# A Mamba block's last chunk finished row tile by row tile, and the graph attention's first adjacency loaded ahead of its branch

## The chip, the cores and the metric

The kernel runs on one core of a Trainium2 chip. The metric is the device time of one execution in microseconds (us); lower is better. The core has TensorE (PE, with its weight loads shown apart as PEld), VectorE (DVE), ScalarE (ACT), GpSimd (POOL) and SyncE (SP), whose queue issues the transfers from memory. Each engine works through its own instructions in order and waits for others by semaphores.

## What is computed

Four graph layers over n = 3327 nodes with 256 features, each of the form x = layernorm(x + layer(x, adj)). All is float32. The second layer (a graph convolution followed by a Mamba scan) and the third (graph attention) are the two between which the change lies:

```python
# layer 1
h = layernorm(relu(adj @ x @ gcn_w + gcn_b))
xz = h @ w_in;  xc, z = xz[:, :512], xz[:, 512:]
u = silu(causal_conv4(xc));  dt, B, C from u @ w_xp
h_t = exp(dt*A) * h_(t-1) + dt*B*u          # a scan over the 3327 nodes, 16 states
y = (h_t @ C + u * D_skip) * silu(z)
x = layernorm(x + y @ w_out)
# layer 2
h = x @ W.T;  a_src = (h*attn_src).sum(-1);  a_dst = (h*attn_dst).sum(-1)
s = leaky_relu(a_src[None, :] + a_dst[:, None], 0.2) * (adj > 0)
w = softmax of s over the neighbours only
x = layernorm(x + elu(w @ h))
```

Layer 0 is an aggregation with a linear map. Layer 3 runs two steps of diffusion with the adjacency and of a bilinear attention (queries and keys of 64 features) that keeps the top 0.9 of each row's probability.

## The kernel before

The nodes are padded to 3328, that is 26 row tiles of 128. X holds the features of all tiles in SBUF for the whole run, F is a second array of the same size that holds the layer's values, and col holds each node's two attention terms. A tile framework places the buffers, sets the semaphores, and orders each engine's instructions; memory of a closed pool is used again by later pools, and an instruction that writes into such memory waits for its last users.

**The Mamba block.** The scan runs over chunks of up to 512 nodes (WC), four row tiles in the last one. For each of 16 states, `decay`, `feed` and `scan` work on ScalarE, GpSimd and VectorE, and TensorE sums the states in PSUM (line 557). The function `gate` (489 to 491) multiplies the sum with the gate. `back` (493 to 519) then finishes a chunk: for each row tile a matmul with w_out in four parts (line 502), the residual into X (504) and its statistics (505, lines 84 and 85 of the helper); then one reciprocal root for the tiles of the chunk on GpSimd (`power`, lines 249 and 250, and 509, 510), and the normalization on ScalarE (514). For all chunks but the last this lies beside the scan of the next chunk. For the last, lines 575 to 579 run it to its end, and then `values` (332 to 350) for its four tiles: two transposes of X (341), a copy (343), the product with the attention's weights (346), and from it col (347) and F (349, 350). Sums, transposes and products all use the two PSUM buffers "ps" of one pool.

**The graph attention** has two forms. Lines 675 to 709 prepare it: they test whether the scores are small enough for the fast form (`fit`), compute q, eps and r, and a branch at 754 chooses `layer2` (711 to 752) or `layer2_any`. In `layer2` each of the 26 rows of tiles comes in two halves of 13 tiles (JH): a load of the transposed adjacency (724), the weights w as a maximum of r and q (726), the mask (729), which writes the weighted half into the load's buffer, and 13 matmuls (732). Each float32 matmul stands as two records in the trace. The row is finished by 737 to 751, the last step on GpSimd (L593, L594, L751), and `project` of the row before (L101, L103, and L600, L602, L604 in `key_and_query`) makes its key and query; the query goes to memory (qd, line 606).

**The last layer** begins behind the branch with loads of U1 and U2 (763) and of the rows ln3 (764), of queries (1108) and of adjacency thirds (807, in `aggregated`), the scores (793), a search for each row on VectorE, and the diffusion's matmuls (809). Some of these loads do not depend on the attention, and where their memory is free they are issued before the branch.

Of the kernel before, what the change touches and what calls it, by code (L numbers as in the profile page):

```python
# [9 lines left out]
F32 = mybir.dt.float32  # L10
BF16 = mybir.dt.bfloat16
I32 = mybir.dt.int32
AF = mybir.ActivationFunctionType
ALU = mybir.AluOpType
# [4 lines left out]
P = 128  # L19
D = 256  # L20
EPS = 1e-5
JH = 13
J0 = 4
JC = 9
WC = 512
DI = 512
NG = DI // P
# [16 lines left out]
def gnn_kernel(ctx: ExitStack, tc: tile.TileContext, n: int, a: dict, out: bass.AP):  # L44
    nc = tc.nc
    nt = -(-n // P)
# [35 lines left out]
    def stats(mv, y):  # L82
        st = small.tile([P, 6], F32, name="bnst")
        nc.vector.bn_stats(st, y)  # L84
        nc.vector.bn_aggr(mv, st)
# [68 lines left out]
    with tc.tile_pool(name="l1b", bufs=1) as wpool, tc.tile_pool(name="l1at", bufs=2) as l1at:  # L154
        X0 = F[:, :, :D]
# [32 lines left out]
        with tc.tile_pool(name="l1aw", bufs=1) as cwork, tc.tile_pool(name="l1c", bufs=2) as ch, \  # L188
# [58 lines left out]
            def power(rs, var):  # L247

                nc.gpsimd.tensor_scalar(rs, var, EPS, None, op0=ALU.add)
                nc.gpsimd.tensor_tensor(rs, rs, mhalf[:, :var.shape[1]], op=ALU.pow)  # L250
# [237 lines left out]
            def gate(c, ys):  # L488
                sz = szs[c]
                for g in range(NG):  # L490
                    nc.vector.tensor_mul(sz[:, g, :], ys[g][:, :sz.shape[2]], sz[:, g, :])

            def back(c):

                sz = szs[c]
                m = sz.shape[2] // P
                mv = small.tile([P, WC // P, 2], F32, name="mvc")
                for i in range(m):
                    it = starts[c] // P + i
                    po = psum.tile([P, WC], F32, name="ps")[:, :D]  # L500
                    for g in range(NG):
                        nc.tensor.matmul(po, sz[:, g, i * P:(i + 1) * P], w_out[:, g, :],
                                         start=(g == 0), stop=(g == NG - 1))
                    nc.vector.tensor_add(X[:, it, :], X0[:, it, :], po)
                    stats(mv[:, i, :], X[:, it, :])
                rs = small.tile([P, WC // P], F32, name="rsc")
                power(rs[:, :m], mv[:, :m, 1])
                nb = small.tile([P, WC // P], F32, name="nbc")
                nc.gpsimd.tensor_tensor(nb[:, :m], mv[:, :m, 0], rs[:, :m], op=ALU.mult)
                nc.gpsimd.tensor_scalar(nb[:, :m], nb[:, :m], -1.0, None, op0=ALU.mult)  # L510
                yield
                for i in range(m):
                    it = starts[c] // P + i
                    x = nc.scalar.activation(X[:, it, :], X[:, it, :], AF.Identity, scale=rs[:, i:i + 1], bias=nb[:, i:i + 1])
                    if i == 0:
                        tc.keep_in_program_order(x)
                nonlocal ready
                ready = ends[c] // P
                yield
# [53 lines left out]
                if c + 1 < nch:  # L573
                    x = y
            gate(nch - 1, ys)
            for _ in back(nch - 1):
                pass
            while valued < nt:
                values()

# [3 lines left out]
    with tc.tile_pool(name="l3", bufs=1) as pool, tc.tile_pool(name="l3d", bufs=1, space=DRAM) as dram:  # L584
# [89 lines left out]

        with tc.tile_pool(name="l2c", bufs=1) as cpool:
            fit = cpool.tile([1, 1], I32, name="fit")
            with tc.tile_pool(name="l2a", bufs=1) as wpool, \
                    tc.tile_pool(name="l2p", bufs=3, space=PSUM) as psum:

                big = wpool.tile([P, nt, 2], F32, name="big")  # L680
                nc.scalar.activation(big, col, AF.Abs)
                m = wpool.tile([P, 2], F32, name="m")
                nc.vector.reduce_max(m, big.rearrange("p t k -> p k t"), axis=AX.X)
                pm = psum.tile([2, P], F32, name="ps")
                nc.tensor.transpose(pm, m, ident)
                m2 = wpool.tile([2, 1], F32, name="m2")
                nc.vector.reduce_max(m2, pm, axis=AX.X)
                one = wpool.tile([2, 1], F32, name="one")
                nc.vector.memset(one, 1.0)
                ps = psum.tile([1, 1], F32, name="ps")  # L690
                nc.tensor.matmul(ps, m2, one, start=True, stop=True)
                f = wpool.tile([1, 1], F32, name="f")
                nc.vector.tensor_scalar(f, ps, BIG, None, op0=ALU.is_le)
                nc.vector.tensor_copy(fit, f)

                q = cpool.tile([P, nt], F32, name="q")
                nc.scalar.activation(q, col[:, :, 0], AF.Exp, scale=0.8)
                eps = cpool.tile([P, nt], F32, name="eps")
                nc.scalar.activation(eps, col[:, :, 1], AF.Exp, scale=-1.0)
                nc.vector.tensor_scalar_mul(eps, eps, 1e-8)  # L700

                r = cpool.tile([P, npad], F32, name="r")
                for j0 in range(0, nt, 4):
                    m = min(4, nt - j0)
                    pt = psum.tile([P, 4, P], F32, name="ps")
                    for j in range(m):
                        nc.tensor.transpose(pt[:, j, :], col[:, j0 + j, 1:2].to_broadcast([P, P]), ident)
                    nc.scalar.activation(r[:, j0 * P:(j0 + m) * P], pt[:, :m, :].rearrange("p a b -> p (a b)"),
                                         AF.Exp, scale=-0.8)

            def layer2():
                with tc.tile_pool(name="l2", bufs=1) as pool, tc.tile_pool(name="l2w", bufs=2) as work, \
                        tc.tile_pool(name="l2at", bufs=5) as atp, \
                        tc.tile_pool(name="l2p", bufs=3, space=PSUM) as psum:
                    def project(it):
                        xt = transposed(work, psum, X[:, it, :], "xt")
                        key_and_query(work, psum.tile([P, P], F32, name="ps"), 0, it, xt)

                    for it in range(nt):
                        acc = psum.tile([P, D + 1], F32, name="acc")  # L720
                        for j0 in range(0, nt, JH):
                            m = min(JH, nt - j0)
                            at = atp.tile([P, JH, P], F32, name="at")
                            nc.sync.dma_start(at[:, :m, :], a["adjT"][it][:, j0:j0 + m, :])
                            w = work.tile([P, JH, P], F32, name="w", bufs=1)
                            nc.vector.tensor_tensor(
                                w[:, :m, :], r[:, None, it * P:(it + 1) * P].to_broadcast([P, m, P]),
                                q[:, j0:j0 + m, None].to_broadcast([P, m, P]), op=ALU.max)
                            nc.vector.scalar_tensor_tensor(at[:, :m, :], at[:, :m, :], 0.0, w[:, :m, :],  # L729
                                                           op0=ALU.is_gt, op1=ALU.mult)  # L730
                            for j in range(m):
                                nc.tensor.matmul(acc, at[:, j, :], F[:, j0 + j, :],  # L732
                                                 start=(j0 + j == 0), stop=(j0 + j == nt - 1))
                        if it:
                            project(it - 1)
                        den = small.tile([P, 1], F32, name="den")
                        nc.vector.tensor_add(den, acc[:, D:], eps[:, it:it + 1])
                        nc.vector.reciprocal(den, den)

                        ex = work.tile([P, D], F32, name="ex")  # L740
                        nc.vector.tensor_scalar(ex, acc[:, :D], den, 0.0, op0=ALU.mult, op1=ALU.min)
                        nc.scalar.activation(ex, ex, AF.Exp)
                        o = work.tile([P, D], F32, name="o")
                        nc.scalar.activation(o, acc[:, :D], AF.Relu, scale=den)
                        nc.vector.scalar_tensor_tensor(o, ex, -1.0, o, op0=ALU.add, op1=ALU.add)
                        nc.vector.tensor_add(o, o, X[:, it, :])
                        mv = small.tile([P, 2], F32, name="mv")
                        stats(mv, o)
                        rs = small.tile([P, 1], F32, name="rs")
                        power(rs, mv)  # L750
                        nc.gpsimd.tensor_scalar(X[:, it, :], o, mv[:, 0:1], rs, op0=ALU.subtract, op1=ALU.mult)  # L751
                    project(nt - 1)

            with tc.If(nc.values_load(fit[0:1, 0:1]) > 0) as small_scores:
                layer2()
            with small_scores.Else():
                layer2_any()
# [573 lines left out]
```

## Time and profile before

| | |
|---|---|
| device time, median of 3 | 3858.1 us (3853.97 to 3861.62) |
| span of the profiled execution | 3854.7 us |
| first matmul of the last chunk's w_out | 1617.68 us |
| last col of `values` | 1641.42 us |
| first attention matmul (L732) | 1652.72 us |
| last L600 of the attention starts | 1988.46 us |
| first diffusion matmul of the last layer (L809) | 1992.59 us |

A line of the timeline has the start and the duration in us, the engine, the source line, the operation, "output <- inputs" with shapes, and in brackets how long the engine had been idle before it and what ended that. A line of the waits has who waited for whom, the total in us, how often, and the longest. A line of the windows has the stretch, its length, the busy time of PE, PEld, DVE, ACT and POOL with the number of instructions, the clock that was granted to TensorE (1.00 is full), the share of the DMA engines and GB/s.

### The profile page before, as it was taken

To read this page: it belongs to the slowest core of one execution; us is meant where nothing else is said; L and a number is where in the kernel's file an instruction comes from. 1 tells how busy PE (TensorE), PEld (TensorE's weight loads), DVE (VectorE), ACT (ScalarE), POOL (GpSimd) and SP (SyncE) were. 2 spreads that over 40 slices of the span, in tenths; PEclk is the share of its full clock that TensorE was granted. 3 is DMA by queue.
4 is the path that set the end of the run, shared out by engine and by line. 5 is a ranking of instruction groups with operands and counts; after the bars stand their busy time and mean duration, and the time that the engine had idled before them with its cause. 6 is when DMAs were issued, how large, how long until landed. Compare 5 with 4: busy or idle time off the path is not lost. (4 is left out here: it accounts for less than half of the span.)

```text
span 3854.7 us, 41751 instructions
## 1 busy us (share of the span) xinstructions
PE 3499.9 (91%) x15079; PEld 2593.0 (67%) x15079; DVE 2610.2 (68%) x5588; ACT 1738.5 (45%) x2612; POOL 494.7 (13%) x734
## 2 busy tenths in 40 slices
PE   8999999898889778689989999999999999999975
PEld 7888876554554434378868787777777667667664
DVE  1111579898988999877753445444454888888987
ACT  0000665554545465211122333333346777777773
POOL 0000122222221221111110000000001111111110
PEclk9999999998999888889999999999999999999997
DMA  7443211111111000044423222122203112221100
GB/s 231 139 134 95 84 59 53 37 46 36 42 36 36 6 0 0 15 158 139 148 73 88 62 61 56 51 59 62 59 11 101 58 56 63 64 63 54 58 23 7
DMA packets 100529, 252.96 MB, mean 66 GB/s; under 512 B 14786, under 2 KB 49090, under 8 KB 100178
## 3 DMA queue, kind: packets, MB, share of 16 engines
q1 hardware_dynamic: 100306, 250.13, 21.2%
q8 instruction: 122, 2.00, 0.2%
q14 instruction: 101, 0.83, 0.1%
HBM read 239.86 MB, written 10.22 MB: 65 GB/s over the span
## 5 line engine op out<-in xcount | busy, mean ns | idle before, releaser
L473 DVE TENSOR_TENSOR_SCAN h<-dA,db 128x2052 f32<-128x2052 f32 (+3 forms) x128 | 464.0, 3625 | 5.9 <-PE y L557 3.4
L460 ACT ACTIVATE dA<-dt,A_log 128x512 f32<-128x512 f32 (+3 forms) x512 | 297.0, 637 | 326.7 <-DVE h L473 272.7
L557 PE MATMUL y<-h,ident 128*128 128x512 f32 (+3 forms) x1024 | 436.1, 563 | 3.2 <-DVE h L549 3.2
L841 PE MATMUL acc<-G,wt 128*128 128x256 f32 x1352 | 332.7, 396 | 63.4 <-ACT wt L839 62.2
L557 PEld LDWEIGHTS y<-h,ident 128*128 128x128 f32 x1024 | 199.4, 207 | 258.0 <-issue 232.4
L839 ACT COPY wt<-tp 128x512 f32<-128x512 f32 (+1 forms) x364 | 185.9, 554 | 382.7 <-PE tp L837 382.4
L841 PE MATMUL acc<-X,wt 128*128 128x256 f32 x1352 | 343.8, 391 | 10.3 <-ACT wt L839 9.8
L841 PEld LDWEIGHTS acc<-G,wt 128*128 128x128 f32 x1352 | 254.1, 194 | 133.7 <-ACT wt L839 81.6
L809 PE MATMUL acc<-F,at 128*128 128x256 f32 x1352 | 323.1, 389 | 0.6 <-ACT q L604 0.6
L116 PE MATMUL acc<-xa,at 128*128 128x257 f32 x1352 | 310.1, 383 | 5.4 <-DMA at<-in_adjT 5.4
L841 PEld LDWEIGHTS acc<-X,wt 128*128 128x128 f32 x1352 | 242.3, 189 | 105.5 <-issue 41.3
L732 PE MATMUL acc<-F,at 128*128 128x257 f32 x1352 | 307.9, 384 | 4.9 <-DVE at L729 4.9
L264 PE MATMUL cb<-F,at 128*128 128x256 f32 x1352 | 310.6, 382 | 1.6 <-ACT hn L283 1.6
L809 PE MATMUL acc<-X,at 128*128 128x256 f32 x1352 | 309.4, 383 | 2.9 <-issue 2.9
L809 PEld LDWEIGHTS acc<-F,at 128*128 128x128 f32 x1352 | 253.8, 193 | 74.0 <-issue 40.0
L264 PEld LDWEIGHTS cb<-F,at 128*128 128x128 f32 x1352 | 257.3, 191 | 58.7 <-issue 17.7
L466 DVE TENSOR_TENSOR db<-du,row 128x2048 f32<-128x2048 f32 (+3 forms) x128 | 240.2, 1879 | 82.6 <-ACT row L448 82.5
L853 DVE MAX8 cand<-e 128x8 f32<-128x128 f32 x676 | 142.2, 281 | 226.4 <-ACT e L795 214.9
L116 PEld LDWEIGHTS acc<-xa,at 128*128 128x128 f32 x1352 | 256.7, 192 | 42.6 <-issue 5.4
L809 PEld LDWEIGHTS acc<-X,at 128*128 128x128 f32 x1352 | 255.0, 192 | 44.0 <-issue 10.9
L732 PEld LDWEIGHTS acc<-F,at 128*128 128x128 f32 x1352 | 256.4, 193 | 41.8 <-issue 5.1
L549 DVE TENSOR_TENSOR h<-h,C 128x2048 f32<-128x2048 f32 (+3 forms) x128 | 240.9, 1882 | 37.2 <-PE C L484 23.7
(305 smaller groups left out, 5303.6 us busy)
## 6 DMA issues: line engine op xcount, KB each, us to landing
at<-in_adjT SPq DMA_DIRECT2D x102, 832.0 KB, 4.5
at<-in_adjT SPq DMA_DIRECT2D x156, 448.0 KB, 3.4
at<-in_adjT SPq DMA_DIRECT2D x52, 576.0 KB, 3.8
at<-in_adjT SPq DMA_DIRECT2D x52, 320.0 KB, 3.0
at<-in_adjT SPq DMA_DIRECT2D x26, 512.0 KB, 3.5
xt<-in_xT SPq DMA_DIRECT2D x26, 128.0 KB, 4.1
qd<-q SPq DMA_DIRECT2D x104, 32.0 KB, 1.9
q<-qd SPq DMA_DIRECT2D x52, 64.0 KB, 2.3
```

The lines of the kernel that those rows point to most:

```text
L116: nc.tensor.matmul(acc, at[:, j, :], rhs[:, j0 + j, :], start=(j0 + j == 0), stop=(j0 + j == nt - 1))
L264: nc.tensor.matmul(acc, at[:, j % JC, :], X0[:, j, :], start=(j == 0), stop=(j == nt - 1))
L460: nc.scalar.activation(dA[:, g, 1:], dt[:, g, :], AF.Exp, scale=A[:, g, s:s + 1])
L466: nc.vector.tensor_mul(by_group(dbs[s % 2], w)[:, :, 1:], du, B.to_broadcast([P, NG, w]))
L473: nc.vector.tensor_tensor_scan(h[:, :m], dAs[s % 2][:, :m], dbs[s % 2][:, :m], initial=0.0, op0=ALU.mult, op1=ALU.add)
L549: nc.vector.tensor_mul(h, h, C.to_broadcast([P, NG, w]))
L557: nc.tensor.matmul(ys[g][:, :w], ident, h[:, g, :], start=False, stop=(s == DS - 1))
L732: nc.tensor.matmul(acc, at[:, j, :], F[:, j0 + j, :], start=(j0 + j == 0), stop=(j0 + j == nt - 1))
L809: nc.tensor.matmul(acc, at[:, j, :], rhs[:, j0 + j, :], start=(j0 + j == 0), stop=(j0 + j == nt - 1))
L839: nc.scalar.copy(wt[:, :m, :], pt[:, :m, :])
L841: nc.tensor.matmul(acc, wt[:, j, :], rhs[:, j0 + j, :], start=(j0 + j == 0), stop=(j0 + j == nt - 1))
L853: nc.vector.max(cand[:, s * 8:(s + 1) * 8], z[:, s * SEG:(s + 1) * SEG])
```

## The change

It has two parts. The last chunk is no longer finished by `back`: a loop takes each row tile through its sum, statistics, reciprocal root and normalization by itself, with `values` of the tile before it in between, so that a tile need not wait for the other three. And the two halves of the attention's first row of adjacency get buffers of their own, at0 and at13, in the pool that is open before the branch, and are loaded there; row 0 uses them, and the pool for the other rows has four buffers instead of five. The sum of a tile has become a function of its own, which `back` uses too.

```diff
+            def residual(c, i):
+                it = starts[c] // P + i
+                po = psum.tile([P, WC], F32, name="ps")[:, :D]
+                for g in range(NG):
+                    nc.tensor.matmul(po, szs[c][:, g, i * P:(i + 1) * P], w_out[:, g, :],
+                                     start=(g == 0), stop=(g == NG - 1))
+                nc.vector.tensor_add(X[:, it, :], X0[:, it, :], po)
...
             gate(nch - 1, ys)
-            for _ in back(nch - 1):
-                pass
+            for i in range(us[nch - 1].shape[2] // P):
+                it = starts[nch - 1] // P + i
+                residual(nch - 1, i)
+                mv = small.tile([P, 2], F32, name="mv")
+                stats(mv, X[:, it, :])
+                rs, nb = (small.tile([P, 1], F32, name=x) for x in ("rs", "nb"))
+                power(rs, mv[:, 1:2])
+                nc.gpsimd.tensor_scalar(nb, mv[:, 0:1], rs, -1.0, op0=ALU.mult, op1=ALU.mult)
+                nc.scalar.activation(X[:, it, :], X[:, it, :], AF.Identity, scale=rs, bias=nb)
+                while valued < ready:
+                    values()
+                ready = it + 1
             while valued < nt:
                 values()
...
             fit = cpool.tile([1, 1], I32, name="fit")
+            ats = [cpool.tile([P, min(JH, nt - j0), P], F32, name=f"at{j0}") for j0 in range(0, nt, JH)]
+            for k, at in enumerate(ats):
+                nc.sync.dma_start(at, a["adjT"][0][:, k * JH:k * JH + at.shape[1], :])
...
-                        tc.tile_pool(name="l2at", bufs=5) as atp, \
+                        tc.tile_pool(name="l2at", bufs=4) as atp, \
...
-                            at = atp.tile([P, JH, P], F32, name="at")
-                            nc.sync.dma_start(at[:, :m, :], a["adjT"][it][:, j0:j0 + m, :])
+                            if it:
+                                at = atp.tile([P, JH, P], F32, name="at")
+                                nc.sync.dma_start(at[:, :m, :], a["adjT"][it][:, j0:j0 + m, :])
+                            else:
+                                at = ats[j0 // JH]
```

More of the change, by code (lines that the diff above doesn't have):

```diff
@@ L491, in gate @@
                     nc.vector.tensor_mul(sz[:, g, :], ys[g][:, :sz.shape[2]], sz[:, g, :])
+            def residual(c, i):
[5 more added lines that the diff above has]
+                nc.vector.tensor_add(X[:, it, :], X0[:, it, :], po)
             def back(c):
-                sz = szs[c]
-                m = sz.shape[2] // P
+                m = szs[c].shape[2] // P
                 mv = small.tile([P, WC // P, 2], F32, name="mvc")
                 for i in range(m):
[L499 to L505, printed above, removed]
+                    residual(c, i)
+                    stats(mv[:, i, :], X[:, starts[c] // P + i, :])
                 rs = small.tile([P, WC // P], F32, name="rsc")
```

## The prediction

> **What bounds the kernel now.** I read the busy table first, then the chain of waits, then the waits of TensorE alone from the change to the end of the graph attention (1624 to 1990 us), then the timeline around each of them, and last the windows of 1 us with the granted clock.
>
> ```profile
> PE 3499.9 (91%) x15079; PEld 2593.0 (67%) x15079; DVE 2610.2 (68%) x5588; ACT 1738.5 (45%) x2612; POOL 494.7 (13%) x734
> ...
> PE ps L101 <- POOL X L751: 15.3, 3, 6.3
> PE acc L732 <- DVE at L729: 4.9, 1, 4.9
> PE ps L341 <- ACT X L514: 3.9, 1, 3.9
> ```
>
> TensorE is busy 91%, and the chain covers only the last stage, so it says nothing here. The change lies between two stages in which TensorE is nearly full, so what counts is TensorE's idle and slow time in between. The three waits are the ones to explain.
>
> ```profile
> 1617.68 7.07 PE L502 MATMUL ps<-w_out,sz 128*128 128x256 f32 x32
> 1625.70 0.18 DVE L85 BATCH_NORM_AGGREGATE mvc<-bnst 128x2 f32<-128x6 f32 x1
> 1627.98 2.08 ACT L514 ACTIVATE X<-X,nbc,rsc 128x256 f32<-128x256 f32 x4 [31.72 <-POOL nbc L510]
> 1628.63 0.44 PE L341 MATMUL ps<-ident,X 128*128 128x128 f32 x2 [3.89 <-ACT X L514]
> 1639.30 2.09 PE L346 MATMUL ps<-wg,m 128*128 128x258 f32 x4 [0.46 <-ACT m L343]
> 1641.42 0.16 ACT L347 COPY col<-ps 128x2 f32<-128x2 f32 x1 [1.80 <-PE ps L346]
> 1644.27 46.70 SPq L724 DMA_DIRECT2D at<-in_adjT  x10
> 1644.94 1.89 DVE L726 TENSOR_TENSOR w<-r,q 128x1664 f32<-128x1664 f32 x1 [1.41 <-PE ps L707]
> 1650.68 1.89 DVE L729 SCALAR_TENSOR_TENSOR at<-at,w 128x1664 f32<-128x1664 f32 x1 [3.85 <-DMA at<-in_adjT]
> 1652.72 30.04 PE L732 MATMUL acc<-F,at 128*128 128x257 f32 x128 [4.90 <-DVE at L729]
> ```
>
> The four row tiles of the last chunk go through in lockstep: all sums, one power for four, four normalizations, then four times "values" (L341, L346) one behind the other. The first mask (L729) then waits 3.85 us for its load, which is issued only after the branch.
>
> ```profile
> 1683.11 4.54 POOL L594 TENSOR_TENSOR rs<-rs,mhalf 128x1 f32<-128x1 f32 x1 [0.21 <-POOL rs L593]
> 1687.77 1.24 POOL L751 TENSOR_SCALAR X<-o,mv,rs 128x256 f32<-128x256 f32 x1
> 1689.07 0.69 PE L101 MATMUL ps<-ident,X 128*128 128x128 f32 x2 [6.31 <-POOL X L751]
> ```
>
> Row 0's projection stands in TensorE's queue after 64 of the attention's matmuls and waits 6.31 us for X.
>
> ```profile
> 1628.00:1629.00 1.00, 0.36 (x2) 0.20 (x2) 0.00 (x0) 1.00 (x3) 0.00 (x0) 1.00 0.00 0
> ...
> 1630.00:1631.00 1.00, 0.64 (x2) 0.54 (x3) 0.00 (x0) 0.31 (x2) 0.00 (x0) 0.50 0.00 0
> ```
>
> The third figure from the end is the granted clock (the last two are the DMA share and GB/s): after the idle 3.9 us it falls to 0.50 and stays there until 1646.5, so the values run at half speed.
>
> ```profile
> 1992.59 5.96 PE L809 MATMUL acc<-X,at 128*128 128x256 f32 x14 [2.91 <-issue]
> 1992.82 1.97 SPq L1108 DMA_DIRECT2D q<-qd  x2
> 1998.48 0.97 PE L793 MATMUL sc<-kT,q 64*128 64x416 f32 x4
> ```
>
> At the start of the last layer, seven matmuls of L809 run before the scores. Their adjacency had been loaded at 1617.91, ahead of the branch.
>
> **What the Trainium skill says.** "TensorE: Matmul & The Clock Gate", Part 1: the clock is either half or full and is decided in free-running windows of about 3.4 us by how busy the array was. The trace agrees: the changes at 1629.4, 1646.5, 1649.95, 1656.7, 1687.4 and 1694.3 lie on multiples of 3.41 us. Windows busy 49% (1612.4 to 1615.8) and 63% stayed at full clock, one with 40% (1646.5 to 1649.9) fell. "SBUF — State Buffer", Who interferes with whom: a VectorE instruction with two SBUF inputs and a GpSimd instruction that reads SBUF exclude each other for the whole instruction. The trace agrees: L594 takes 0.57 us alone and 4.54 us at 1683.11, while masks and weights (1.89 us each) follow each other on VectorE.
>
> **The change part by part.** *Tail by row tile.* Up to 1617.68 the built program has the same order on every engine. Then TensorE's order is sum 0, sum 1, values 0, sum 2, values 1, sum 3, values 2, values 3. A sum is 7.07/4 = 1.77 us. Row 0: add and statistics end at 1620.70, as now; 0.27 to GpSimd, then 0.22 (L249), 0.57 (L250, 128x1) and 0.27 (the row of the same form, L292) with gaps 1.25 together: ScalarE normalizes at 1622.2, TensorE follows 0.65 later (now 1627.98 to 1628.63): 1622.9 instead of 1628.63. TensorE then idles only 1.7 us, so I take the full clock: values cost 0.38 + 0.5 (copy L343) + 0.9 = 1.8 us instead of 2.97. Values 0 to 1624.7, sum 2 to 1626.45, values 1 to 1628.25, sum 3 to 1630.0, values 2 to 1631.8. Row 3: its sum at 1630.0 + 1.2 + 0.27 + 1.25 + 0.65 = 1633.4, its L346 at 1634.3, its col at 1635.3, now 1641.42: 6.1 earlier. The two PSUM buffers that sums and values share come free in time (F of row 0 ends near 1625.8, before 1626.45). At half clock in row 3 it is 1.2 less; with half clock from row 0 on, sums too, some 4 less. Extra work, three more powers on GpSimd and single nb's, lies beside the matmuls of the other rows.
>
> *Loads ahead of the branch.* The waits of the two loads resolve to the last L346 (wg's memory is reused), so they start at about 1635.3, not at once. A lone load of this kind lands after 4.5 us (the DMA table): 1639.8. The weights w start 3.5 us after col (1641.42 to 1644.94 now): 1638.8, end 1640.7. So the load is just hidden, the mask ends at 1642.6 and TensorE starts there instead of 1652.72: 10.1 earlier in all, 8.8 with a half-clock row 3.
>
> *Row 0's projection* now stands after 52 matmuls, and VectorE's row 0 work before mask 7. From TensorE's start P: the first mask starts at P-1.95 and den comes 17.2 us after it, as now (1650.68 to 1667.90): P+15.3. Two weights and a mask (1.93 each) and the small operations put the end of the statistics at P+22.9. GpSimd's last step meets mask 7, whose load lands near P+23.7, and X is normalized at P+26.8. TensorE arrives at P+24.9 (52 x 0.4416 + 1.9 for four half-clock microseconds): it idles 1.9 us. Now it loses 6.3 plus 2.6 (5.2 us at half clock after 1689.07) = 8.9. With an even chance of a clock drop I book 2.7: gain 6.2.
>
> *Four buffers instead of five.* A tile takes TensorE 5.98 us; its buffer is freed, loaded in 4.5 and masked within 8, needed 17.9 later. Both orders issue a load at mid-row and one at the row's end, so the wait is where it was. No cost, but the slack of X against L101 is only some 0.3 us per row.
>
> *Start of the last layer.* The memory moves, and so that three adjacency loads, U2 and the two rows ln3 now stand behind the branch: U2 and the rows ahead of q, the adjacency after it. TensorE's first act is the scores. The transfers ahead of q landed in 3.6 to 5.8 us before (the DMA table), so I put q's landing where the first scores stand now, near 1998; no trace shows it. By then TensorE has done nothing where it did seven matmuls (7 x 0.44 = 3.1 us), and the first two rounds of scores run at half clock, some 2 us: cost 5, between 3 and 6.5.
>
> Sum: -10.1 - 6.2 + 5 = -11.3: 3858.1 to 3846.8, rounded 3847.
>
> **The rivals.** *A: a second stall goes as well.* At 1746.4 TensorE waits 4.04 us for X and then runs slow, 6.4 in all, because one load landed after 6.1 instead of 4.5 us and GpSimd's turn then met a mask. The change does not aim at it, but it is an accident of timing that the new phase may miss: 3840.4. Against: late landings can recur elsewhere.
> *B: clock and port go against it.* Tail at half clock (start 6 earlier), row 0's projection blocked as long as now: -6 + 0 + 5 = -1: 3857. For: GpSimd was held four instructions long in this very place.
> *C: slower.* With X just in time each row, a load or mask later by 0.6 us costs 24 rows x 0.6 = 14.4: -11.3 + 14.4: 3861. For: slack is 0.3 us; against: the timing of loads is by TensorE's releases, the same in both.
>
> **How the numbers follow.** Main 0.47, A 0.30, B 0.13, C 0.10. Nearly all of main and A, and little of B, is more than 0.2% (7.7 us) faster: 0.78; same 0.13, slower 0.09, which takes in all of C but a little. The range leaves out C and half of B above, and goes below A by the 3 us of an L3 start that costs little and a projection without a wait: 3835 to 3855.
>
> **What would show it.** Right: the last col near 1635; no DMA wait at the first mask; the first attention matmul near 1643; the wait before the first L101 under 3 us; scores before L809 in the last layer. Wrong: the granted clock at 0.50 from 1630 on; GpSimd's power over 2 us again; a DMA wait over 3 us in every row.

## The result, and the profile after

The changed kernel takes 3840.8 us (median of four runs, 3835.4 to 3844.8) against 3856.4 us for the kernel before in the same session; the ratio is 0.9957, 95% interval 0.994 to 0.9974. It was timed again later (e6 below): 3842.4 us, ratio 0.9966 [0.9953, 0.998]. So it is 0.2 to 0.6% faster, some 13 to 16 us, by both.

The page's busy table of the changed kernel, and TensorE's waits between 1624 and 1974 us (total, times, longest):

```profile
PE 3482.4 (91%) x15079; PEld 2577.9 (67%) x15079; DVE 2610.2 (68%) x5588; ACT 1737.7 (45%) x2612; POOL 492.4 (13%) x742
...
PE ps L101 <- POOL X L772: 12.6, 3, 5.5
PE ps L346 <- ACT m L343: 2.0, 4, 0.6
PE acc L753 <- DVE at L750: 1.3, 1, 1.3
```

The line numbers have moved: L498 is the sum of a row tile (L502 before), L588 its normalization (L514), L747, L750 and L753 are weights, mask and matmul of the attention (L726, L729, L732), L772 is X (L751), L607 and L608 are the power (L593, L594), L614 the key and query projection (L600), L814 and L830 scores and aggregation of the last layer (L793, L809), L858 the first transposes of the scores (L837). The wait for the mask has fallen from 4.9 to 1.3 us. The waits for X have not gone: 15.3 has become 12.6.

The timeline of TensorE in the tail:

```profile
1617.69 3.62 PE L498 MATMUL ps<-w_out,sz 128*128 128x256 f32 x16
1622.73 0.44 PE L341 MATMUL ps<-ident,X 128*128 128x128 f32 x2 [1.42 <-ACT X L588]
1623.64 1.14 PE L346 MATMUL ps<-wg,m 128*128 128x258 f32 x4 [0.46 <-ACT m L343]
1624.61 1.89 PE L498 MATMUL ps<-w_out,sz 128*128 128x256 f32 x8
...
1634.24 1.14 PE L346 MATMUL ps<-wg,m 128*128 128x258 f32 x4 [0.61 <-ACT m L343]
```

Two sums, then values 0 after 1.42 us of idling instead of 3.89, then sums and values in turn. An L346 takes 1.14 us instead of 2.09: the clock stays up. In the windows of 1 us (the third figure from the end is the granted clock):

```profile
1630.00:1631.00 1.00, 0.48 (x3) 0.20 (x2) 0.85 (x3) 0.47 (x2) 0.00 (x0) 1.00 0.00 0
...
1638.00:1639.00 1.00, 1.00 (x7) 1.00 (x6) 0.16 (x1) 0.60 (x1) 0.00 (x0) 0.50 0.95 386
...
1640.00:1641.00 1.00, 1.00 (x12) 1.00 (x10) 0.97 (x2) 1.00 (x3) 0.00 (x0) 1.00 1.01 426
```

The clock falls only after the tail, and is full again by 1640, before the attention begins. The timeline of all engines from the last col on:

```profile
1635.42 0.16 ACT L347 COPY col<-ps 128x2 f32<-128x2 f32 x1 [1.23 <-PE ps L346]
1635.55 0.80 SPq L694 DMA_DIRECT2D at<-in_adjT  x2
...
1638.84 1.89 DVE L747 TENSOR_TENSOR w<-r,q 128x1664 f32<-128x1664 f32 x1 [1.41 <-PE ps L725]
1640.77 1.89 DVE L750 SCALAR_TENSOR_TENSOR at<-at,w 128x1664 f32<-128x1664 f32 x1
```

The loads are issued 0.13 us after col, and the mask L750 follows the weights with no wait for DMA (3.85 us before). TensorE's first attention matmul comes at 1642.81:

```profile
1642.81 22.84 PE L753 MATMUL acc<-F,at 128*128 128x257 f32 x104 [1.31 <-DVE at L750]
1671.14 0.69 PE L101 MATMUL ps<-ident,X 128*128 128x128 f32 x2 [5.49 <-POOL X L772]
```

52 matmuls (x104) pass without a gap, and row 0's projection then waits 5.49 us for X. On GpSimd the power (L607, L608) is what is long. Its two instructions stand beside a mask and weights of VectorE:

```profile
1665.51 1.87 DVE L750 SCALAR_TENSOR_TENSOR at<-at,w 128x1664 f32<-128x1664 f32 x1
1665.74 1.71 POOL L607 TENSOR_SCALAR rs<-mv 128x1 f32<-128x1 f32 x1 [33.23 <-PE acc L753]
1667.41 1.89 DVE L747 TENSOR_TENSOR w<-r,q 128x1664 f32<-128x1664 f32 x1
1667.54 2.19 POOL L608 TENSOR_TENSOR rs<-rs,mhalf 128x1 f32<-128x1 f32 x1
1669.84 1.24 POOL L772 TENSOR_SCALAR X<-o,mv,rs 128x256 f32<-128x256 f32 x1
```

And the start of the last layer, TensorE and two of SyncE's loads:

```profile
1972.33 1.22 PE L614 MATMUL ps<-xt,wkq 128*128 128x128 f32 x4 [0.52 <-ACT xt L103]
1975.83 0.35 SPq L68 DMA_DIRECT2D U<-in_U  x1
...
1977.58 1.58 SPq L1129 DMA_DIRECT2D q<-qd  x1
...
1981.96 1.76 PE L814 MATMUL sc<-kT,q 64*128 64x416 f32 x4 [8.41 <-DMA q<-qd]
1983.65 2.93 PE L830 MATMUL acc<-X,at 128*128 128x256 f32 x6
```

U2 and the two rows are loaded here, ahead of q, as predicted. The scores come first and wait for q; they and the first aggregation run at half clock (0.50 from 1980 to 1988).

### The profile page after: what moved, and what is told of

It reads as the page before. It is cut to its first block, busy times and chain, and to the rows that moved or that the text cites. A ratio compares the mean times of both kernels' runs of the same rounds, so it can differ in the third digit from the quotient of the medians.

```text
span 3838.5 us, 41766 instructions
## 1 busy us (share of the span) xinstructions
PE 3482.4 (91%) x15079; PEld 2577.9 (67%) x15079; DVE 2610.2 (68%) x5588; ACT 1737.7 (45%) x2612; POOL 492.4 (13%) x742
## 5 line engine op out<-in xcount | busy, mean ns | idle before, releaser
L830 PE MATMUL acc<-F,at 128*128 128x256 f32 x1352 | 317.2, 384 | 0.6 <-ACT q L618 0.6
L830 PE MATMUL acc<-X,at 128*128 128x256 f32 x1352 | 306.9, 381 | 0.0
L753 PE MATMUL acc<-F,at 128*128 128x257 f32 x1352 | 304.2, 381 | 1.3 <-DVE at L750 1.3
L830 PEld LDWEIGHTS acc<-F,at 128*128 128x128 f32 x1352 | 248.9, 189 | 72.0 <-issue 39.4
L830 PEld LDWEIGHTS acc<-X,at 128*128 128x128 f32 x1352 | 253.3, 191 | 40.7 <-issue 7.1
L753 PEld LDWEIGHTS acc<-F,at 128*128 128x128 f32 x1352 | 253.7, 191 | 37.0 <-issue 1.5
```

The source lines that it names most:

```text
L753: nc.tensor.matmul(acc, at[:, j, :], F[:, j0 + j, :], start=(j0 + j == 0), stop=(j0 + j == nt - 1))
L830: nc.tensor.matmul(acc, at[:, j, :], rhs[:, j0 + j, :], start=(j0 + j == 0), stop=(j0 + j == nt - 1))
```

## The experiments

One trace of each kernel is not enough here: the first residual sum of the last chunk begins anywhere between 1614.5 and 1623.7 us in these traces, though nothing before it was changed in any of them. So I read stretches, each from its own mark: from the first residual sum to the last col and to the first attention matmul; from there to the last key and query projection; from there to the first transposes of the scores in the last layer; and from there to the end. All in us:

```
                   first sum to          first attention   last projection   from there
                   last col  first att.  to last proj.     to first transp.  to the end
before             23.74     35.04       335.74            81.12             1785.1
e5 before again    23.73     36.29       332.41            78.71             1786.4
changed            17.73     25.12       329.52            83.61             1782.6
e6 changed again   17.73     25.11       325.35            84.31             1785.2
e1 tail only       17.73     30.24       327.45            78.87             1786.2
e2 loads only      23.73     31.21       325.20            83.63             1783.6
e3 warm lockstep   20.81     27.89       324.66            84.86             1785.3
e4 four buffers    23.72     36.07       328.92            78.65             1786.3
e7 projection late 17.73     25.12       316.94            83.68             1784.1
e8 q first         17.73     25.17       327.01            82.19             1785.4
e9 no mask         17.72     25.94       322.24            83.59             1784.0
e10 both additions 17.74     25.92       316.94            81.57             1784.6
```

**e1, the tail alone.** The loads of the first row go back behind the branch:

```diff
-            ats = [cpool.tile([P, min(JH, nt - j0), P], F32, name=f"at{j0}") for j0 in range(0, nt, JH)]
...
-                        tc.tile_pool(name="l2at", bufs=4) as atp, \
+                        tc.tile_pool(name="l2at", bufs=5) as atp, \
...
```

> Only the tail by row tile; the first adjacency is loaded behind the branch and the pool has five buffers, as in the kernel before. Theory (tail and loads each give their own part): last col at 1635.4 as in the changed kernel, the first mask still waits for its load (issue near 1638.2 plus the 6.4 us that it took before, plus 1.9 for the mask), first attention matmul near 1646.7 instead of 1652.7 and 1642.8. The start of the last layer as before (seven aggregation matmuls ahead of the scores, 81 us from the end of the attention to the first transposes of the scores). Time about 6 us below before. Rival (the tail alone brings all): first matmul under 1644, time 12 us or more below before.

Measured: 3847.0 us, ratio to before 0.9978 [0.9972, 0.9985]. The tail gives its 6.0 us in full, but the first attention matmul comes only 4.8 (against the first trace of before) or 6.05 (against the second) earlier; expected were 6.0. The timeline of e1 shows what is left:

```profile
1641.44 0.16 ACT L347 COPY col<-ps 128x2 f32<-128x2 f32 x1 [1.23 <-PE ps L346]
1641.55 0.81 SPq L68 DMA_DIRECT2D U<-in_U  x2
...
1644.30 3.92 SPq L738 DMA_DIRECT2D at<-in_adjT  x5
1644.97 1.89 DVE L740 TENSOR_TENSOR w<-r,q 128x1664 f32<-128x1664 f32 x1 [1.41 <-PE ps L721]
1651.92 1.89 DVE L743 SCALAR_TENSOR_TENSOR at<-at,w 128x1664 f32<-128x1664 f32 x1 [5.06 <-DMA at<-in_adjT]
```

The load is issued 2.86 us after col, behind the last layer's U1, U2 and two rows, and is there 7.6 us later; VectorE has its weights long before. The theory holds in the main: the tail alone does not bring all, and the wait for the load remains. In this trace, with the attention as it was before, the second stall of rival A is missing.

**e2, the loads alone.** The tail is the old one, the rest as in the changed kernel:

```diff
-            for i in range(us[nch - 1].shape[2] // P):
...
+            for _ in back(nch - 1):
+                pass
```

> Only the loads ahead of the branch with four buffers; the tail in lockstep. Theory: the loads wait for the last L346 and are issued near 1641.5, land 4.5 later, the mask ends near 1648.8 and the first attention matmul follows there instead of at 1652.7: 3.9 earlier. The last layer starts 2.5 later relative to the end of the attention, as in the changed kernel (83.6 instead of 81.1 us to its first transposes). Time 1 to 4 us below before, if row 0's projection is blocked as long as before. Rival (the loads bring nothing without the tail): first matmul at 1651 or later, time not below before.

Measured: 3849.5 us, ratio 0.9989 [0.9983, 0.9996]. The first attention matmul comes 3.8 us earlier than in the first trace of before, as expected, and 5.1 earlier than in the second. From the last col to it there are 7.48 us (31.21 - 23.73), as in the changed kernel (7.39) and not as before (11.3 and 12.6). The last layer's start is 83.63, the longer one. The rival falls. Log ratios of e1 and e2 add to 0.33%, beside 0.43 and 0.34% for both parts together.

**e3, the old order with a warm TensorE.** To e2 this adds, between the last sum and the first values, nine matmuls whose result nobody reads:

```diff
+            warm = cpsum.tile([P, 2, D], F32, name="cb")
+            for i in range(9):
+                tc.keep_in_program_order(nc.tensor.matmul(warm[:, 0, :], szs[nch - 1][:, 0, :P], w_out[:, 0, :],
+                                                          start=True, stop=True))
```

> The changed kernel with the old tail in lockstep and nine matmuls that nobody reads between the last residual sum and the first values, so that TensorE is busy where it stood idle for 3.9 us. Theory (most of the tail's 6 us is the clock): the clock stays at 1.00, the four values take 1.8 us each instead of 3.0, last col near 1636, first matmul near 1643.4, time within 2 us of the changed kernel. Rival (the order brings it, by starting the values earlier): last col after 1639.5, time 4 to 6 us above the changed kernel.

Measured: 3843.9 us, ratio 0.9973 [0.9963, 0.9983]. That is 1.5 and 3.1 us above the changed kernel's two medians, which were timed apart. From first sum to last col it is 20.81 us: neither 18 to 19 (all four values at full clock) nor 23.7, so neither the theory nor the rival holds as it stood. The timeline shows the first of the values fast and the second slow, and a stretch of 1 us that the clock has fallen:

```profile
1635.13 1.14 PE L346 MATMUL ps<-wg,m 128*128 128x258 f32 x4 [1.29 <-ACT m L343]
...
1637.02 1.95 PE L346 MATMUL ps<-wg,m 128*128 128x258 f32 x4 [0.53 <-ACT m L343]
...
1638.00:1639.00 1.00, 1.00 (x5) 0.70 (x3) 0.00 (x0) 0.00 (x0) 0.00 (x0) 0.50 0.00 0
```

The third value's L346 takes 1.49 us and the fourth's 1.14 again. So the values in lockstep, with their waits for ScalarE's copies, do not hold the clock even after a warm start: in the 3.4 us before it fell TensorE was busy 47%. The clock accounts for at least 2.9 of the 6.0 us (23.7 - 20.81), since the first values begin 10.9 us after the first sum in e3 as in before. The other 3.1 are the order together with the clock that it holds, since the sums between the values fill their gaps; the two are not separable further by this run.

**e4, four buffers alone.** The kernel before with one number changed:

```diff
-                        tc.tile_pool(name="l2at", bufs=5) as atp, \
+                        tc.tile_pool(name="l2at", bufs=4) as atp, \
```

> The kernel before with four adjacency buffers instead of five and nothing else. Theory (no cost): the rows of the attention keep their period of 11.97 us, TensorE's waits between 1652 and 1990 are those of before within 1 us a row, time within 3 us of before. Rival (fewer buffers hold back the loads): VectorE waits for more loads than before, single rows over 12.5 us, time 5 us or more above before.

Measured: 3853.4 us, ratio 0.9995 [0.9986, 1.0004]: no cost. TensorE's two waits for X inside the attention were shorter in its trace (4.75 and 1.85 us), by more than the 1 us that I had allowed. The order has changed here: with four buffers row 0's projection stands after 52 matmuls, as in the changed kernel, and the power takes 1.80 and 2.19 us. With five, in before and e1, it stands after 64, and the power's second instruction takes 4.54 and 4.44 us. So it is the number of buffers that moves row 0's projection, not the loads ahead of the branch. The last layer's start is the short one (78.65), so the fourth buffer is not what lengthens it.

**e5 and e6, both kernels once more.** No edit.

> The kernel before once more, unchanged, for a second trace of it. It tells how far the attention's length (first attention matmul to the last key and query projection: 335.7 us before, 329.5 after, 325 to 329 in the first four experiments) belongs to the order of the instructions. Theory (the second stall at 1746 was an accident of one execution): the attention lasts 325 to 331 us this time, and most of the 6.2 us between the two traces there does not belong to the change. Rival (it belongs to the order before): 335 to 336 us again, with two stalls.

> The changed kernel once more, unchanged, timed beside the kernel before. Theory: tail 17.7 us from the first residual sum to the last col, first attention matmul 25.1 after that sum, row 0's projection waits 5 to 6 us for GpSimd, attention 325 to 330 us, 83.6 us from there to the first transposes of the scores; ratio 0.994 to 0.997. Rival (the 16 us between the first two traces hold for any execution): ratio at or below 0.9957 again and attention at 329.5.

Measured: before again 3851.2 us (one run), changed again as told above. The theory of e5 falls in its main point: the second stall is there again at 1748.87, 3.90 us long, and the attention takes 332.4 us, above the 331 that I had allowed and below the rival's 335. In the changed kernel the place shows 2.20 us in the first trace and nothing in the second. Row 0's wait repeats closely: 6.31 and 6.82 before, 5.49 and 5.49 after. The theory of e6 holds in each number within 1 us, the ratio included.

**e7, each projection a row later.** To the changed kernel:

```diff
-                        if it:
-                            project(it - 1)
+                        if it > 1:
+                            project(it - 2)
...
+                    project(nt - 2)
                     project(nt - 1)
```

> The changed kernel with each row's key and query projected a row later (two projections after the last row). Theory (what remains between 1642 and 1972 is TensorE waiting for GpSimd's X, held by VectorE's masks): the waits of 5.49 and 2.20 us and the slow clock after them (about 3 us) go, the attention's length falls from 329.5 to about 319, time 8 to 11 us below the changed kernel; at the end 4.9 us of wait for the last X stay. Rival (masks or loads bound the attention as well): attention over 324 us, VectorE's loads or masks ending last instead, time less than 5 us below the changed kernel.

Measured: 3834.6 us, ratio 0.9945 [0.9931, 0.9958]; the changed kernel, timed beside it, had 3842.4, so it is 7.8 less by the medians, just short of the 8 to 11 expected. The attention takes 316.94 us. TensorE's waits in e7, from 1640 to 1970 us:

```profile
PE ps L101 <- POOL X L772: 2.9, 1, 2.9
PE ps L614 <- ACT xt L103: 2.1, 3, 1.0
```

Of the waits for X only the last is left (2.9 us; I had expected 4.9). GpSimd is as slow in row 0 as it was (1.72, 2.19 and 1.24 us), but nobody stands behind it. Loads and masks do not take the place: the rival falls.

**e8, the first query ahead of the other loads.** To the changed kernel: U1, U2 and the two rows get their tiles where they were, and their transfers are written after the first scores' query and the first loads of the aggregation:

```diff
-        u1, u2 = (load(pool, x) for x in ("U1", "U2"))
-        g3, b3 = (load_row(pool, x) for x in ("ln3_g", "ln3_b"))
+        u1, u2 = (pool.tile(list(a[x].shape), F32, name=x) for x in ("U1", "U2"))
+        g3, b3 = (pool.tile([P, D], F32, name=x) for x in ("ln3_g", "ln3_b"))
...
+                    if i == 0:
+                        for x, t in (("U1", u1), ("U2", u2)):
+                            tc.keep_in_program_order(nc.sync.dma_start(t, a[x]))
...
```

> The changed kernel with the first query, and the aggregation's first three loads, issued ahead of U1, U2 and the two rows of the last layer norm after the branch. Theory (the late start of the last layer is q's load behind the others): q is issued about 1.7 us earlier and lands within 3 us, scores begin 6 to 7 us after the last key and query projection instead of 9.6, and the first transposes of the scores 80.5 instead of 83.6 us after it; time 3 us below the changed kernel. Rival (q waits for the branch and its own write to DRAM): scores at 9 us or later, no gain.

Measured: 3839.6 us, ratio 0.9957 [0.9942, 0.9972], against e6's 0.9966 [0.9953, 0.998]: too close to tell apart. The trace does tell: first scores 7.45 us after the last projection instead of 9.63 and 10.33, first transposes 82.19 instead of 83.61 and 84.31. The gain is 1.4 to 2.1 of the expected 3: the query's load is issued 4.39 us after that projection instead of 5.25, so 0.9 us earlier and not 1.7, since the query's own write to memory has to land first.

**e9, two VectorE instructions taken out.** The kernel leaves out the mask and the weights that follow row 0's statistics on VectorE, so that row 3 computes other numbers:

```diff
+                            if (it, j0) != (3, JH):
+                                w = work.tile([P, JH, P], F32, name="w", bufs=1)
...
+                            if (it, j0) != (3, 0):
+                                nc.vector.scalar_tensor_tensor(at[:, :m, :], at[:, :m, :], 0.0, w[:, :m, :],
...
```

> The changed kernel without two VectorE instructions of two SBUF inputs that follow row 0's statistics: row 3's first half keeps its adjacency unmasked, and its second half is masked with the weights of the first (so this row's numbers are others). Theory (these two instructions hold GpSimd): behind row 0's statistics L607 takes 0.23, the power 0.57 and X 1.24 us as in later rows, X is there 2.1 us after the statistics instead of 5.7, and TensorE's wait at row 0's projection falls from 5.5 to about 2 us. Rival (GpSimd is slow in row 0 because it is its first work after a pause of 33 us): 1.7 and 2.2 us again, the wait stays at 5.5.

Measured: 3841.1 us (one run); what counts is the timeline of VectorE and GpSimd in it:

```profile
1671.27 0.18 DVE L85 BATCH_NORM_AGGREGATE mv<-bnst 128x2 f32<-128x6 f32 x1
1671.61 0.22 POOL L607 TENSOR_SCALAR rs<-mv 128x1 f32<-128x1 f32 x1 [33.37 <-DVE mv L85]
1672.08 0.57 POOL L608 TENSOR_TENSOR rs<-rs,mhalf 128x1 f32<-128x1 f32 x1 [0.25 <-POOL rs L607]
...
1674.06 0.44 PE L101 MATMUL ps<-ident,X 128*128 128x128 f32 x2 [1.85 <-POOL X L774]
...
1677.10 1.86 DVE L752 SCALAR_TENSOR_TENSOR at<-at,w 128x1664 f32<-128x1664 f32 x1
1677.27 1.78 POOL L607 TENSOR_SCALAR rs<-mv 128x1 f32<-128x1 f32 x1 [3.26 <-DVE mv L85]
1679.00 1.89 DVE L748 TENSOR_TENSOR w<-r,q 128x1664 f32<-128x1664 f32 x1
1679.13 2.18 POOL L608 TENSOR_TENSOR rs<-rs,mhalf 128x1 f32<-128x1 f32 x1
```

After the same pause of 33 us the power is as short as in later rows, and TensorE waits 1.85 us instead of 5.49. In row 1, where a mask and weights now stand behind the statistics, the same two instructions take 1.78 and 2.18 us: each ends with the VectorE instruction beside it. That decides it against the pause.

**e10, both additions.** The edits of e7 and e8 together.

> Both additions to the changed kernel together: the projection a row later, and the first query ahead of the last layer's other loads. Theory: the two gains add up, attention 317 us, first transposes of the scores 82 us after the last projection; time 10 us below the changed kernel, 22 below before. Rival (q's early landing brings nothing once the attention ends earlier): time as with the later projection alone.

Measured: 3832.0 us, ratio 0.9932 [0.9918, 0.9945]: 26.0 us below before by the medians (22 expected). Beside the changed kernel it was not timed; its median is 8.8 and 10.4 us below that kernel's two. Attention 316.94 and 81.57 us to the first transposes, as the two edits gave singly. Beside e7 alone (0.9945 [0.9931, 0.9958]) the second edit's share is in the trace, and in the time it is not certain.

## Why the prediction was right

The forecast was 3847 in a range of 3835 to 3855, and the time was 3840.8: faster, inside the range, and 6 us below the number. By the prediction's steps, as means of the two traces of each kernel (from the table above where nothing else is said):

*Tail and loads, -10.1 predicted: -10.6.* First sum to last col, predicted 6.1 and measured 6.0; the full clock that I took, and the order of sums and values, are in the trace. From col to the attention 4.5 us less, with the load just hidden as reckoned: mask at 1640.77, predicted 1640.7. e1 and e2 show that the two shares are separate.

*Row 0's projection, -6.2 predicted: about -3.6. This is the step that failed.* Call the first attention matmul P, as the prediction does. The second L101 stands behind the same 78 matmuls in the four traces; it comes at P+45.7 and P+45.2 before and at P+41.8 in both traces after. TensorE was to wait 1.9 us for X; it waits 5.49. That difference of 3.6 us has two parts, and only the smaller one costs time.

The larger part is that TensorE comes to the projection at P+22.8 and not at P+24.9, because the clock was full from the first matmul on. It gains nothing by that, since the projection waits for X in any case. e3 shows it: there the attention begins at half clock, its 52 matmuls take 24.52 us instead of 22.84, the wait is shorter by about as much, and L101 comes at P+28.2, where it comes at P+28.3 in the changed kernel:

```profile
1650.35 24.52 PE L747 MATMUL acc<-F,at 128*128 128x257 f32 x104 [2.26 <-DVE at L744]
1678.53 0.69 PE L101 MATMUL ps<-ident,X 128*128 128x128 f32 x2 [3.65 <-POOL X L766]
```

The other part is X itself, which was to be there at P+26.8 and came 1.5 us later. I had L594's long turn moved onto X (L772), beside a mask. Instead the first mask after the statistics held L607, and the weights right behind it held L608. The prediction cited "SBUF — State Buffer", Who interferes with whom, for the lock; e9 shows that it acts here, on the mask (a scalar_tensor_tensor with two SBUF inputs) as on the weights. What was wrong was the count: I let one of GpSimd's three instructions be blocked, and two were. In e3 the mask starts 0.4 us after the statistics, since it waits for its load, and the two blocked are the power's second instruction and X (2.20 and 2.49 us). After the wait TensorE runs at half clock until 1674, which costs 1.5 us where I had booked an even chance of it. The prediction's sign of being wrong, GpSimd's power over 2 us again, was there: 2.19.

*What made up for it.* The attention as a whole came out 6.6 us shorter (334.1 to 327.4), close to the 6.2, but by another way, and that is luck. Row 0 gives about 3.6 of it. Most of the rest is rival A come true in part: the second stall was 4.04 and 3.90 us before, and is 2.20 in one trace after and absent in the other. With the slow clock behind it, it lengthens the rows (the time from one L101 to the next, undisturbed 11.97 us) by 6.8 and 4.1 us before and by 4.1 and 0.2 after, 3.3 less in the mean. Rival A's 3840.4 is thus near the measured time, but by a different sum. Why the second stall goes is not settled: e1, e2, e3 and e8 each lack it, four buffers alone halve it (one trace), so it seems to hang on the phase of loads and masks, which every edit shifts. This is argued, not shown.

*Four buffers, 0 predicted:* no cost in e4, where the 95% interval reaches from 5.4 us faster to 1.5 slower. Rival C (a wait in every row) fails: nearly all rows of the changed kernel take 11.97 to 12.2 us.

*The start of the last layer, +5 predicted: +4.0.* The two first traces gave +2.5; the second pair gave +5.6. The four traces in which the last layer's first adjacency is loaded ahead of the branch (before, e5, e1, e4) and those in which it is not fall into two groups that do not overlap: 78.7 to 81.1, and, where q is not first, 83.6 to 84.9. The scores begin 9.6 and 10.3 us after the last projection, before 10.0 and 9.3; what is missing is the seven matmuls that stood ahead of them, and the clock is at half in the first scores, as predicted.

*The rest, not in the prediction: -1.9.* From the first transposes to the end it is 1785.1 to 1786.4 us in those four traces and 1782.6 to 1785.4 in the others, so some 2 us of the late start seem to come back later. Where, I did not find, and the two groups overlap; it stays open whether the start's net cost is 4 or 2.

Together these are -15.1, and the spans of the four traces differ by 15.5 (3852.0 to 3836.5 in the mean). That agrees with the 13 to 16 us of the medians.

## What to carry to other kernels

When one stage hands row tiles to the next, interleave the last tiles of the first with the first of the second: the gain is the shorter wait, and also the clock, which the filled gaps hold up. A load moved ahead needs memory, and something else pays for it: here the early loads brought 4.5 us, and a second set of loads lost its place ahead of the branch, which took back 2 to 4 of them. When a consumer waits for a small chain on an engine that can be locked out, count every instruction of the other engine that the chain may meet; or move the consumer a row later (e7), which here took the wait away though the chain stayed as slow, with no work added. And a shorter wait is a gain only if what it waits for comes earlier as well.

## What the runs showed that I had not expected

A 128x1 instruction of GpSimd, 0.23 us alone, takes 1.71 to 1.84 us beside a mask or weights, and one of 0.57 mostly 2.19; in the changed kernel and in e9 each of them ends within 0.5 us after the VectorE instruction that it met. TensorE's clock came back to 1.00 by 1640 in the changed kernel while it did nothing but float32 transposes (from 1637.00 on, busy 1.00 in the two microseconds before), while in e3 it fell between 1637 and 1638, some 4 us after nine matmuls in a row. Nor does the busy share of a window, as the prediction read it, tell by itself what follows: in the changed kernel TensorE was busy 54% from 1633.1 to 1636.5 and the clock fell, and busy 53% from 1663.8 to 1667.2 and it stayed; why is open. And the traces differ by 9 us in when the last chunk's tail begins, though the work up to there is the same, and single stretches differ by 2 to 4 us between two traces of one kernel: the first pair showed 2.5 us for the start of the last layer, the second 5.6.
